# When the next field is split: eleven of the fields' halves moved within the row before their own

## The chip, the cores and the metric

The kernel runs on one core of one Trainium2 chip. The metric is the device time of one execution in microseconds, given as the median of several runs; one further execution of the same program was profiled instruction by instruction.

## The reference

The input is `r_inputs`, 1024 samples x 32 fields x 128 values, and `W`, one 128 x 128 matrix for each of the 496 pairs of fields (i, j) with i < j. All are 32-bit floats.

```python
v_i = inputs[:, I_IDX, :]
v_j = inputs[:, J_IDX, :]
transformed = jnp.einsum('bpd,ped->bpe', v_i, W)
return transformed * v_j
```

For each pair, field i is multiplied by the pair's matrix, and the product by field j, element by element. The output has 1024 x 496 x 128 values, 260 MB, against some 49 MB that are read.

## The kernel before

Pairs are numbered q in an order that goes by rows: field i = 30 comes first with its one pair, then i = 29 with two, down to i = 0 with 31. "Row i" below means the 31 - i pairs whose first field is i; `first_q[i]` is the number of its first pair. A pair is worked in two halves of 512 samples; u = 2q + half counts them.

Rows 30 to 26 (the first 15 pairs) are computed by one 32-bit matmul each half (line 212). In all others each factor is split into a coarse part and a rest, so that three fast matmuls give a half: `wh` with `xh` and `wl` with `xl` (line 215), and `wd` with `xd` (line 224), which is added three halves later (`LAG`). Between them ScalarE scales what has been accumulated (line 216). VectorE multiplies the result by field j into the output tile `ot` (line 230).

The splits are made while the kernel runs:

- A weight split (`split_w`, for two pairs) is one instruction on ScalarE (line 127) and three on GpSimd (lines 128, 129, 130).
- A field split (`split_x`, for half a field) is one on ScalarE (line 144, `xh`), and on GpSimd lines 145 and 146 (`xl`) and, for fields 9 to 0, line 150 (`xd`). For fields 25 to 10, `xd` is made on VectorE instead, five pairs later (line 269).

The order is written out by hand, and each engine works through its own instructions in that order. A list, `todo`, holds every split with the pair from which it may be issued and the pair by which it's due; it is sorted by the due pair. After each pair the first entry that may be issued is issued, one at a time (lines 260 to 264). A weight split may be issued from five pairs ahead of its use. A half of field i may be issued from `first_q[i + 1] + 1`, the beginning of the row before its own, and is due at `first_q[i]`:

```python
todo.append(((c - 3) * WC + 1, max(c * WC, nq0), lambda u, c=c: split_w(c, u)))
```

A weight split becomes due at every second pair, and those stand first in the list, so the two halves of a field take the two next free places: for field 5, pairs 302 and 304, with one weight split between them. Its row begins at pair 325, and the row in which it is split, row 6, at 300. The split tiles `xh`, `xl`, `xd` have two buffers each: field i is written over field i + 2.

Output goes out in tiles of four pairs, 2 MB each, issued by ScalarE's queue (line 259) two halves after the tile's last multiplication. There are three tiles of their own (`s0` to `s2`), and up to four more, which are the places of the four groups of late fields (`g0` to `g3`) for as long as these aren't loaded. A group of four fields (2 MB) is loaded at pairs 52, 141, 219 and 313 (line 108), and its place isn't used for output from 20 pairs before that; from pair 293 on three tiles are left. VectorE may write a tile again when its store has landed.

Weights come in chunks of eight pairs (512 KB) into three buffers, some by SyncE's queue alone (line 118), 25 of them in two parts, by GpSimd's queue (line 102) and SyncE's (line 103). A very small DMA (`mark`, line 99) follows these on GpSimd's queue. Field 0 is loaded at pair 421 into a weight buffer (line 90).

Of the kernel before, what the change touches and what calls it, by code (L numbers as in the profile page):

```python
# [12 lines left out]
NF = 32  # L13
# [7 lines left out]
NATIVE = 5  # L21
SHARED = 16
XDLAG = 10
LAG = 3
WB = 3
WLEAD = 12
XAFTER = 54
# [18 lines left out]
def kernel(  # L46
# [27 lines left out]
    spool = ctx.enter_context(tc.tile_pool(name="xs", bufs=2))  # L74
    rpool = ctx.enter_context(tc.tile_pool(name="wr", bufs=WB))
    wpool = ctx.enter_context(tc.tile_pool(name="ws", bufs=4))
# [5 lines left out]
    def load_x(f, pieces=1, eng=None):  # L82
        if f == 0:

            t = rpool.tile([P, WL, P], F32, tag="w", name="x_0").rearrange("p q e -> p (q e)")
        else:
            t = xpool.tile([P, BT], F32, tag=f"x{f}", name=f"x_{f}")
        s = BT // pieces
        for k in range(pieces):
            (eng or nc.sync).dma_start(out=t[:, k * s : (k + 1) * s], in_=xt[f, :, k * s : (k + 1) * s])  # L90
        x_sb[f] = t
# [20 lines left out]
    def load_w(c, splits=(0, WL), eng=nc.sync):  # L112
        w_raw[c] = rpool.tile([P, WL, P], F32, tag="w", name=f"w_{c}")
        if c in WAPART:
            load_apart(w_raw[c], wt[c])
            return
        for a, b in zip(splits, splits[1:]):
            eng.dma_start(out=w_raw[c][:, a:b, :], in_=wt[c, :, a:b, :])
# [19 lines left out]
    def split_x(f, a, u):  # L138

        if a == 0:  # L140
            x_s[f] = [spool.tile([P, BT], F32R, tag=t, name=f"{t}_{f}") for t in ("xh", "xl", "xd")]
        s = slice(a, a + HB)
        h, l, d = [t[:, s] for t in x_s[f]]
        nc.scalar.mul(h, x_sb[f][:, s], 1.0 - 2.0**-13)  # L144
        nc.gpsimd.tensor_tensor(l, x_sb[f][:, s], h.bitcast(F32), ALU.subtract)  # L145
        nc.gpsimd.tensor_scalar(l, l.bitcast(F32), 1.0 / EPS, 1.0, ALU.mult, ALU.mult)  # L146
        if f > NF - 2 - NATIVE - SHARED:
            later.append((min(u + XDLAG, 2 * first_q[f] + LAG - 1), d, h.bitcast(F32), l.bitcast(F32)))
        else:
            nc.gpsimd.tensor_tensor(d, h.bitcast(F32), l.bitcast(F32), ALU.subtract)  # L150
# [3 lines left out]
    first_q = {i: q for q, (i, j) in reversed(list(enumerate(pairs)))}  # L154
# [3 lines left out]
    todo = []  # L158
    for c in range(c0, nchunk):
        todo.append(((c - 3) * WC + 1, max(c * WC, nq0), lambda u, c=c: split_w(c, u)))  # L160
    for i in range(NF - 2 - NATIVE, -1, -1):
        for a in range(0, BT, HB):
            todo.append((first_q[i + 1] + 1 if i < NF - 3 - NATIVE else 2, first_q[i], lambda u, i=i, a=a: split_x(i, a, u)))
    todo.sort(key=lambda t: t[1])

    load_w(0, (0, 1, WL), nc.sync)
# [10 lines left out]
    w_at = {}  # L177
    for c in range(WB, -(-NQ // WL)):
        free = (c - WB + 1) * WL if (c - WB) * WL < nq0 else 0
        early = 0 if XAFTER < c <= XAFTER + WB else WLEAD - 6  # L180
        if c not in WAPART:
            w_at[max(c * WL - 3 * WC - 5 - early, free)] = c
    x_at = XAFTER * WL - 11
    assert x_at not in w_at and len(w_at) == NQ // WL - WB - len(WAPART)

# [32 lines left out]
    def second(u):  # L218
        q, h = divmod(u, 2)
        i, j = pairs[q]  # L220
        r = slice(q % WC * P, (q % WC + 1) * P)
        s = slice(h * HB, (h + 1) * HB)
        if q >= nq0:
            nc.tensor.matmul(  # L224
                po[u], w_s[q // WC][2][:, r], x_s[i][2][:, s], start=False, stop=True, skip_group_check=True
            )
        g, k = divmod(q, OG)
        if k == 0 and h == 0:
            ots[g] = out_tile(g)
        nc.vector.tensor_tensor(ots[g][:, k, s], po.pop(u), x_sb[j][:, s], ALU.mult)  # L230
        if q >= NQ - 2:
            stores.append((u + SLAG, out[g, :, k, s], ots[g][:, k, s]))
        elif g == 0 or q >= NQ - OG:
            if h == 1:
                stores.append((u + SLAG, out[g, :, k], ots[g][:, k]))
        elif k == OG - 1 and h == 1:
            stores.append((u + SLAG, out[g], ots[g]))

    for u in range(2 * NQ + LAG + SLAG):
        q = u // 2  # L240
        if u < 2 * NQ:
            i, j = pairs[q]
# [11 lines left out]
            if u == 2 * x_at + 1:  # L254
                load_x(0)
        if LAG <= u < 2 * NQ + LAG:
            second(u - LAG)
        while stores and stores[0][0] <= u - LAG:
            nc.scalar.dma_start(*stores.pop(0)[1:])
        if u % 2 == 1:  # L260
            ready = [t for t in todo if t[0] <= q]
            if ready:
                ready[0][2](u)
                todo.remove(ready[0])
        if w_next and (XAFTER if w_next[0] == XAFTER + 2 else w_next[0] - WB) in spent:
            load_w(w_next.pop(0))
# [36 lines left out]
```

## Time and profile before

| what | value |
|---|---|
| median of 5 runs | 750.47 us (748.31 to 752.86) |
| profiled execution | 749.89 us, span 748.1 us |
| mean granted TensorE clock | 0.986 |
| HBM read, written | 49.29 MB, 260.05 MB |
| mean rate over the span | 414 GB/s |
| store of an output tile, issue to landing (median) | 12.4 us |
| ScalarE, scaling (line 216), mean | 583 ns, 962 times |
| VectorE, output (line 230), mean | 685 ns, 720 times |
| VectorE, `xd` (line 269), mean | 948 ns, 32 times |
| ScalarE, `xh` (line 144), mean | 630 ns, 32 times |
| GpSimd, `xl`, second step (line 146), mean | 694 ns, 52 times |
| GpSimd, `xd` (line 150), mean | 1289 ns, 20 times |

The span goes from the first instruction to the last; the execution has 1.8 us around it. In the profile PE is TensorE's matmuls, PEld its weight loads, DVE is VectorE, ACT ScalarE, POOL GpSimd and SP SyncE; L128 is line 128 of the kernel. A group of instructions is shown with its busy time and the mean of one in ns, then the idle time of its engine just before, and who ended that. In a timeline and in the chain of waits the first number is the start and the second the length, both in us. Matmuls are pipelined: one is shown with 0.39 us, and the next starts 0.23 us after it.

The time of a pair in the trace: row 12 ends at 288.6 us, row 7 at 454.0, row 6 at 495.4, row 2 at 651.6, row 1 at 697.4.

### The profile page before, as it was taken

What the parts mean: (1) busy time and instruction counts of PE and PEld (TensorE: products, weight loads), DVE (VectorE), ACT (ScalarE), POOL (GpSimd) and SP (SyncE); (2) the same over time, 40 slices, a digit from 0 to 9 for tenths busy, and PEclk for the clock granted to TensorE, in tenths of its full rate; (3) what the DMA queues carried; (4) which work ended last, traced back from release to release, by engine and by line L of the source; (5) the groups of instructions that cost most, each with busy time, mean ns of one, the idle gap of its engine ahead of it and who ended that gap; (6) DMA issues with size and microseconds to landing.
All of it is one profiled execution on the core that took longest, in us unless ns stands there. A gap on an engine that the chain in (4) does not pass through costs nothing.

```text
span 748.1 us, 11063 instructions
## 1 busy us (share of the span) xinstructions
PE 700.7 (94%) x2946; PEld 555.3 (74%) x2946; DVE 669.2 (89%) x1024; ACT 626.1 (84%) x1256; POOL 615.3 (82%) x902
## 2 busy tenths in 40 slices
PE   7998999899999999998999989889999999999993
PEld 3576777687787788776787777668788787877882
DVE  4899999899999999986999979789899998888894
ACT  1298989799999999886898878789899898978993
POOL 1789999999999999896988878778888979797660
PEclk9999999999999999999999999999999999999998
DMA  9999999999999999999999999999999999999998
GB/s 346 423 428 427 424 428 428 419 395 419 415 420 420 424 426 424 424 426 416 426 428 423 429 416 396 407 428 407 423 416 421 408 429 406 418 393 402 419 424 328
DMA packets 32941, 310.06 MB, mean 414 GB/s; under 512 B 5104, under 2 KB 5232, under 8 KB 16752
## 3 DMA queue, kind: packets, MB, share of 16 engines
q10 hardware_dynamic: 19584, 261.10, 83.0%
q1 hardware_dynamic: 8864, 36.77, 12.5%
q0 software_dynamic: 4432, 11.48, 4.2%
q8 instruction: 24, 0.39, 0.2%
q14 instruction: 37, 0.30, 0.1%
HBM read 49.29 MB, written 260.05 MB: 414 GB/s over the span
## 4 chain that ended last, share of the span: by engine, by line
PE 72%; DMA 13%; POOL 8%; DVE 3%; issue 1%; ACT 1%; DVEq 0%; ACTq 0%; POOLq 0%
PE po L215 46%; PE po L224 23%; DMA out_dram<-ot 12%; PE po L212 4%; DVE ot L230 3%; POOL wl L128 2%; POOL xd L150 2%; POOL xl L145 1%; POOL wd L130 1%; POOL xl L146 1%; ACT po L216 1%; DMA x<-in_xt_dram 1%; POOL wd L129 1%; DVE xd L269 0%; ACT wh L127 0%
## 5 line engine op out<-in xcount | busy, mean ns | idle before, releaser
L216 ACT ACTIVATE po<-po 128x512 f32<-128x512 f32 x962 | 545.7, 583 | 89.8 <-PE po L215 50.8
L230 DVE TENSOR_TENSOR ot<-po,x 128x512 f32<-128x512 f32 x720 | 467.9, 685 | 47.4 <-DMA out_dram<-ot 21.4
L215 PE MATMUL po<-xl,wl 128*128 128x512 f32 x962 | 379.5, 395 | 20.1 <-POOL wl L128 18.8
L215 PE MATMUL po<-xh,wh 128*128 128x512 f32 x962 | 378.8, 394 | 9.9 <-DVE ot L230 9.8
L224 PE MATMUL po<-xd,wd 128*128 128x512 f32 x962 | 377.1, 392 | 1.8 <-DVE xd L269 1.8
L215 PEld LDWEIGHTS po<-xl,wl 128*128 128x128 f32 x962 | 182.1, 189 | 66.5 <-POOL wl L128 27.1
L128 POOL TENSOR_TENSOR wl<-w,wh 128x256 fp32r<-128x256 f32 x241 | 184.2, 764 | 47.2 <-ACT wh L127 42.9
L215 PEld LDWEIGHTS po<-xh,wh 128*128 128x128 f32 x962 | 182.1, 189 | 53.0 <-DVE ot L230 14.4
L224 PEld LDWEIGHTS po<-xd,wd 128*128 128x128 f32 x962 | 182.1, 189 | 40.8 <-ACT po L216 2.4
L230 DVE TENSOR_TENSOR ot<-po,x_g 128x512 f32<-128x512 f32 x272 | 176.7, 687 | 21.4 <-PE po L224 14.2
L130 POOL TENSOR_TENSOR wd<-wl,wd 128x256 fp32r<-128x256 f32 x241 | 179.3, 744 | 20.1
L129 POOL TENSOR_SCALAR wd<-wh 128x256 fp32r<-128x256 f32 x241 | 99.1, 411 | 20.5
L127 ACT ACTIVATE wh<-w 128x256 fp32r<-128x256 f32 x241 | 99.3, 412 | 6.0 <-DVE ot L230 5.2
L145 POOL TENSOR_TENSOR xl<-x_g,xh 128x512 fp32r<-128x512 f32 x32 | 41.6, 1301 | 5.0 <-DVE ot L230 4.6
L146 POOL TENSOR_SCALAR xl<-xl 128x512 fp32r<-128x512 f32 x52 | 36.1, 694 | 4.6
L145 POOL TENSOR_TENSOR xl<-x,xh 128x512 fp32r<-128x512 f32 x20 | 26.6, 1330 | 15.7 <-ACT xh L144 15.5
L212 PE MATMUL po<-x,w 128*128 128x512 f32 x60 | 29.4, 652 | 4.1 <-DMA x<-in_xt_dram 4.1
L269 DVE TENSOR_TENSOR xd<-xh,xl 128x512 fp32r<-128x512 f32 x32 | 30.3, 948 | 0.2 <-POOL xl L146 0.2
L212 PEld LDWEIGHTS po<-x,w 128*128 128x128 f32 x60 | 12.1, 207 | 20.6 <-issue 13.3
L150 POOL TENSOR_TENSOR xd<-xh,xl 128x512 fp32r<-128x512 f32 x20 | 25.8, 1289 | 1.7
L144 ACT ACTIVATE xh<-x 128x512 fp32r<-128x512 f32 x20 | 12.4, 627 | 11.4 <-DMA x<-in_xt_dram 11.3
L144 ACT ACTIVATE xh<-x_g 128x512 fp32r<-128x512 f32 x32 | 20.2, 630 | 0.0
(7 smaller groups left out, 33.9 us busy)
## 6 DMA issues: line engine op xcount, KB each, us to landing
out_dram<-ot ACTq DMA_DIRECT2D x122, 2048.0 KB, 12.4
w<-in_wt_dram SPq DMA_DIRECT2D x36, 512.0 KB, 10.5
w<-in_wt_dram POOLq DMA_DIRECT2D x25, 448.0 KB, 11.3
x_g<-in_xt_dram SPq DMA_DIRECT2D x4, 2048.0 KB, 18.1
x<-in_xt_dram SPq DMA_DIRECT2D x14, 512.0 KB, 8.9
out_dram<-ot ACTq DMA_DIRECT2D x6, 512.0 KB, 8.8
w<-in_wt_dram SPq DMA_DIRECT2D x26, 64.0 KB, 5.9
x<-in_xt_dram ACTq DMA_DIRECT2D x4, 256.0 KB, 6.0
```

The source lines that it names most:

```text
L127: nc.scalar.mul(h, raw, 1.0 - 2.0**-13)
L128: nc.gpsimd.tensor_tensor(l, raw, h.bitcast(F32), ALU.subtract)
L129: nc.gpsimd.tensor_scalar(d, h.bitcast(F32), EPS, 1.0, ALU.mult, ALU.mult)
L130: nc.gpsimd.tensor_tensor(d, l.bitcast(F32), d.bitcast(F32), ALU.subtract)
L145: nc.gpsimd.tensor_tensor(l, x_sb[f][:, s], h.bitcast(F32), ALU.subtract)
L146: nc.gpsimd.tensor_scalar(l, l.bitcast(F32), 1.0 / EPS, 1.0, ALU.mult, ALU.mult)
L150: nc.gpsimd.tensor_tensor(d, h.bitcast(F32), l.bitcast(F32), ALU.subtract)
L212: nc.tensor.matmul(po[u], w_raw[q // WL][:, q % WL, :], x_sb[i][:, s], start=True, stop=True)
L215: nc.tensor.matmul(po[u], w_s[c][t][:, r], x_s[i][t][:, s], start=t == 0, stop=t == 1)
L216: nc.scalar.mul(po[u], po[u], 1.0 + EPS)
L224: nc.tensor.matmul(po[u], w_s[q // WC][2][:, r], x_s[i][2][:, s], start=False, stop=True, skip_group_check=True)
L230: nc.vector.tensor_tensor(ots[g][:, k, s], po.pop(u), x_sb[j][:, s], ALU.mult)
```

## The change

Until now every half of a field might be issued from one pair after the beginning of the row before its own. Now, for fields 11 to 1, the first half may be issued a fifth of that row later, and the second three fifths of it (a row of `NF - 2 - i` pairs, rounded down). Fields 25 to 12 and field 0 are as before. The due pair, which sets the order of the list, is unchanged, as are the splits themselves.

```diff
+SPREAD = 12
...
-            todo.append((first_q[i + 1] + 1 if i < NF - 3 - NATIVE else 2, first_q[i], lambda u, i=i, a=a: split_x(i, a, u)))
+            at = first_q[i + 1] + 1 if i < NF - 3 - NATIVE else 2
+            if 0 < i < SPREAD:
+                at += (NF - 2 - i) * (1 + 2 * (a > 0)) // 5
+            todo.append((at, first_q[i], lambda u, i=i, a=a: split_x(i, a, u)))
```

The pairs at which the two halves are issued, for some of the fields:

| field | row before begins | own row begins | before | after |
|---|---|---|---|---|
| 11 | 171 | 190 | 172, 174 | 176, 184 |
| 8 | 231 | 253 | 232, 234 | 236, 246 |
| 5 | 300 | 325 | 302, 304 | 306, 316 |
| 3 | 351 | 378 | 352, 354 | 358, 368 |
| 1 | 406 | 435 | 408, 410 | 412, 424 |
| 0 | 435 | 465 | 436, 438 | 436, 438 |

## The prediction

> **What bounds the kernel now.** I read the page, then the windows, the waits and the chain stretch by stretch, then GpSimd's timeline at a row's beginning. First the page:
>
> ```profile
> PE 700.7 (94%) x2946; PEld 555.3 (74%) x2946; DVE 669.2 (89%) x1024; ACT 626.1 (84%) x1256; POOL 615.3 (82%) x902
> GB/s 346 423 428 427 424 428 428 419 395 419 415 420 420 424 426 424 424 426 416 426 428 423 429 416 396 407 428 407 423 416 421 408 429 406 418 393 402 419 424 328
> L128 POOL TENSOR_TENSOR wl<-w,wh 128x256 fp32r<-128x256 f32 x241 | 184.2, 764 | 47.2 <-ACT wh L127 42.9
> ...
> L145 POOL TENSOR_TENSOR xl<-x_g,xh 128x512 fp32r<-128x512 f32 x32 | 41.6, 1301 | 5.0 <-DVE ot L230 4.6
> ```
>
> Two limits lie close together. TensorE is 94% busy, and the DMA moves up to 428 GB/s; I take 426 as its full rate. An output tile (four pairs) and its share of the weights are 2.097 + 0.262 = 2.359 MB, which is 5.54 us at 426. Unhindered compute issues a store every 5.38 to 5.50 us (stores at 510.86, 516.24, 521.74, 527.12 in ScalarE's timeline), 5.44 on average. So the question is where a TensorE stall costs anything. The windows divide the second half:
>
> ```profile
> 355.00:449.00 94.00, 88.63 (x380) 71.85 (x379) 85.04 (x128) 81.31 (x163) 80.79 (x120) 0.98 1.01 425
> 449.00:488.00 39.00, 35.02 (x153) 28.37 (x153) 31.69 (x48) 32.52 (x66) 32.18 (x49) 1.00 0.99 401
> 488.00:651.00 163.00, 156.13 (x683) 127.37 (x683) 148.34 (x229) 145.99 (x294) 138.75 (x208) 1.00 1.01 418
> ```
>
> The columns are the stretch, its length, busy time of TensorE, its weight loads, VectorE, ScalarE and GpSimd, granted clock, DMA share, GB/s. To 449 the DMA is full. From 449 on, where only three output tiles are left, it runs at 401 and 418: there compute is late. The waits of 488 to 650 and the chain of 488 to 651 say what makes it late:
>
> ```profile
> PE po L215 <- POOL wl L128: 5.8, 4, 1.8
> ```
>
> ```profile
> 500.69 1.27 POOL xl L145
> 502.04 0.63 POOL xl L146
> 502.75 1.29 POOL xd L150
> 504.04 0.69 POOL wl L128
> 504.78 0.50 PE po L215
> ```
>
> After one DMA piece that ends at 488.7 the longest pieces of this chain are TensorE and GpSimd alone. Four times, once a row, the chain leaves TensorE for GpSimd's split of the next field. The four gaps in TensorE's timeline are 1.08 (at 503.7), 1.17 (540.5), 1.81 (580.0) and 1.79 us (620.2). GpSimd's own timeline shows the first:
>
> ```profile
> 495.28 1.30 POOL L145 TENSOR_TENSOR xl<-x_g,xh 128x512 fp32r<-128x512 f32 x1
> 496.67 0.62 POOL L146 TENSOR_SCALAR xl<-xl 128x512 fp32r<-128x512 f32 x1
> 497.38 1.30 POOL L150 TENSOR_TENSOR xd<-xh,xl 128x512 fp32r<-128x512 f32 x1
> 498.63 0.74 POOL L128 TENSOR_TENSOR wl<-w,wh 128x256 fp32r<-128x256 f32 x1
> 499.46 0.41 POOL L129 TENSOR_SCALAR wd<-wh 128x256 fp32r<-128x256 f32 x1
> 499.95 0.74 POOL L130 TENSOR_TENSOR wd<-wl,wd 128x256 fp32r<-128x256 f32 x1
> 500.65 1.31 POOL L145 TENSOR_TENSOR xl<-x_g,xh 128x512 fp32r<-128x512 f32 x1
> ```
>
> A field half takes 498.63 - 495.28 = 3.35 us, a weight split 2.02, and a weight split is due every 5.44/2 = 2.72. So GpSimd has 0.70 to spare per weight split; each half makes the weights 3.35 - 0.70 = 2.65 late, two with one weight split between them 5.30. TensorE waited 1.08 here, so the weights' lead covers about 4.2.
>
> **The change, part by part.** Nothing is added or removed. In the built program 22 halves move (fields 11 to 1): ScalarE's L144, GpSimd's L145 and L146, for fields 9 to 1 its L150, and for 11 and 10 two VectorE instructions of L269 each. The order on TensorE and on SyncE's queue is the same, and so are the bytes.
>
> *GpSimd.* In the new order at least four weight splits stand between the halves of each of fields 9 to 1. Four give back 4 x 0.70 = 2.8 us, more than the 2.65 that a half costs, so the weights are never 5.30 late, but 2.65. GpSimd's queue also has its own DMA issues, 0.62 us each for a weight chunk (L102) and 0.63 for the small mark (L99); some fall next to a moved half. Both at once: 2.65 + 0.62 + 0.63 = 3.90, still under 4.2. If that cover were short by 0.3, 18 halves would cost 5.4 us together; I take nothing. The weight chunk that waits behind a half is issued at most 3.35 us later; the page has these chunks landing 11.3 us after issue, and the chunk goes to the buffer of the third one before it, 18 pairs (24 us) ahead of its first split. Nothing follows.
>
> *The new deadline.* The second half is issued at three fifths of the row. For field 1, 30 - 18 = 12 pairs are left, for field 11 eight: 8 x 1.36 = 10.9 us against 3.35 + 2.65. The cover is 4.9 us.
>
> *ScalarE and VectorE.* A half's L144 takes 0.63 us (the page's mean) in a queue with L216 behind it. In row 12 (265 to 289), with both halves at the row's beginning, TensorE was busy 24.00 of 24.00 us; single halves ask less. The same row covers L269, whose mean is 0.95.
>
> *Fields 11 to 6, before 449: nothing.* Rows 9 to 7 have TensorE gaps of 1.01, 1.16 and 1.16 us (361.6, 392.9, 427.0), but stores there land 13.9 to 16.6 us after issue. One store is 2.097 MB / 426 = 4.9 us, so about two lie ahead of it. At 439 the tiles for output fall from four to three and VectorE waits 4.0 us for a store; an earlier compute waits longer for the same landing. The gain is 0, at most the DMA's shortfall, 94 x (426 - 425)/426 = 0.2.
>
> *Field 5, 449 to 488.* A gap of 1.16 us (465.1) goes. The chain again ends in a DMA wait at 488, so it's worth only what the DMA catches up: all of 39 x (426 - 401)/426 = 2.3 us at most, 0 at least. The stretch holds two things that stay: the dip after the halved clock at 444, and the start of the group load (L108, issued at 466.6). I take 0.8.
>
> *Fields 4 to 1, 488 to 651: the term that counts.* From the store at 486.88 to that at 652.91 are 29 stores in 166.03 us. Compute alone would need 29 x 5.44 = 157.8, the DMA (29 x 2.359 + 0.524 for x_0)/0.426 = 161.7. Whichever is longer rules: 166.0 - 161.7 = 4.3 us gained. Its ends: with the DMA at 430, 160.2 and 5.8 gained; at 419, which is what it reached from 512 to 540 with TensorE busy 28.00 of 28.00, 164.4 and 1.6.
>
> *After 651.* Field 0 stays, and with it the gap of 1.81 us at 660.4. Up to that point the DMA moved 163 us x 418 GB/s = 68.1 MB; now 163 - 4.3 = 158.7 us at 426 move 67.6, so 0.5 MB more lies ahead. From 651 to 742 it moved 91 us x 408 = 37.1 MB; 37.6 in the same 91 us are 413 GB/s, which it can do. The gain passes through.
>
> *What speaks against it.* TensorE's gaps don't vanish, some move into longer waits for stores at 441.9 (2.04 us now) and 479.9 (2.82). The granted clock halved four times, after gaps of 1.99, 3.70, 2.04 and 1.81 us, and did not after 2.82, 1.81 and 1.79 (its mean is 0.72 in 442 to 448 and in 660 to 666, 1.00 in 479 to 484). Three windows of 10 us with a halving read 0.83: (1 - 0.83) x 10 = 1.7 us of clock lost, 3.4 us at half. I reckon with one more, at 480, where almost all of it is hidden by queued stores: 0.5.
>
> The Trainium skill (TensorE: Matmul & The Clock Gate, Part 1: The HAM clock gate) says that the clock falls to half after an idle window of about 3.4 us. The length agrees with the 3.4 of this trace; the threshold doesn't, since 1.81 was enough once. By the rule the gap at 480 would grow to 2.82 + 1.16 = 3.98 and halve for certain, and the gaps at 580 and 620 could never have done so; by the trace either is chance.
>
> **Sum.** 0 + 0.8 + 4.3 - 0.5 = 4.6 us. The profiled execution took 749.89 (its span 748.1, and 1.8 around it): 745.3. The median of the five runs is 750.47, 0.6 higher: 745.9.
>
> **Rivals.** *The DMA gives no more than now.* For: 419 GB/s in 512 to 540, without a stall; scattered chunk loads may set that rate. Against: 425 over 355 to 449, with the same loads. Gain 1.6 + 0 - 0.3: 749.2, with 747.5 to 751 around it. That the splits don't separate, say because another wait holds GpSimd, would give 750.5 and counts here; the gaps all follow a pair of halves, which speaks against it.
>
> *Slower: the clock.* With compute ahead, every hitch of the DMA ends in a TensorE gap. Each halving takes 1.7 us, and in 449 to 742 stores are queued for one at a time. The 4.6 us are used up by 4.6/1.7 = 2.7 halvings that aren't hidden; from five on the kernel is slower by 5 x 1.7 - 4.6 = 3.9: 754.4. For: gaps of 1.81 have sufficed. Against: only two group loads and one fall in tiles make long gaps after 300; a queue that is 5.54 against 5.44 makes gaps of 0.1 us.
>
> **How the numbers follow.** The forecast has 0.60, the unchanged DMA rate 0.25, the clock 0.15. The time is the forecast's, 745.9, its own range 742.9 (2.3 + 5.8 gained, less 0.5) to 748. To hold eight in ten the range takes in the second case and the way to the third: 742.9 to 752.0. About 0.5% (3.75 us) is what a measurement of this kernel can tell from no change. Faster by more: 0.60; within: 0.25; slower by more: 0.15.
>
> **What would show it.** Right: from 488 to 651 no TensorE wait on L128 but that of field 0 afterwards, stores 5.5 us apart, more VectorE waiting on stores, 424 GB/s or more, GpSimd's halves apart by four weight splits. The gap at 660 stays; the wait at 441 grows by some 3 us without any cost. Wrong: new waits on L128 in the middle of rows, DMA at 418 in spite of even stores, or more than five halved stretches.

## The result and the profile after

The changed kernel takes 748.54 us (median of 52 runs, 745.12 to 753.15) against 751.20 for the kernel before (94 runs, 746.42 to 756.38; its first five had 750.47). The ratio is 0.9972, with a 95% interval of 0.9962 to 0.9981: 2.1 us faster (1.4 to 2.9), where 4.6 were forecast. The sign was right and the size about half or less. Single executions spread over 8 us and more, and the two profiled ones don't show the gain: the one before had a span of 748.1 us, the one after 748.8 (750.59 as a whole). So the traces are used for how the work runs, and the ratios for how long it takes.

The page of the changed kernel; its lines 129 and 146 are 128 and 145 of the one before:

```profile
PE 703.5 (94%) x2946; PEld 557.7 (74%) x2946; DVE 665.3 (89%) x1024; ACT 625.8 (84%) x1256; POOL 614.7 (82%) x902
GB/s 347 422 428 427 430 425 429 420 396 423 420 419 424 426 424 424 427 419 420 428 425 425 421 417 394 424 406 414 417 417 411 420 416 417 398 404 379 405 431 344
L129 POOL TENSOR_TENSOR wl<-w,wh 128x256 fp32r<-128x256 f32 x241 | 183.6, 762 | 54.2 <-ACT wh L128 49.9
```

GpSimd has the same work and now idles longer in front of it, because it's ahead: line 129 waited 49.9 us for ScalarE, not 42.9. GpSimd's timeline in row 5 shows why. The two halves of field 4 stand apart, and the first has a small DMA issue directly before it:

```profile
504.29 0.63 POOL L100 DMA_DIRECT2D mark<-in_xt_dram  x1
504.95 1.30 POOL L146 TENSOR_TENSOR xl<-x_g,xh 128x512 fp32r<-128x512 f32 x1
...
508.29 0.76 POOL L129 TENSOR_TENSOR wl<-w,wh 128x256 fp32r<-128x256 f32 x1
...
518.38 1.30 POOL L146 TENSOR_TENSOR xl<-x_g,xh 128x512 fp32r<-128x512 f32 x1
```

The waits of 488 to 650 in the changed kernel:

```profile
DVE ot L234 <- DMA out_dram<-ot: 19.5, 18, 2.4
POOL wl L129 <- ACT wh L128: 16.3, 18, 5.0
PEld po L219 <- DVE ot L234: 8.4, 12, 1.7
```

TensorE's waits for the weight split, 5.8 us before, are gone. In their place VectorE waits 19.5 us for stores to land. In the kernel before it had waited 8.1 there:

```profile
DVE ot L230 <- DMA out_dram<-ot: 8.1, 10, 1.9
```

The chain of 488 to 651 says the same; its first line is the share of each line of the kernel:

```profile
by line: DMA out_dram<-ot 46.7%; PE po L219 23.5%; DVE ot L234 14.0%; PE po L228 11.1%; issue 1.5%; POOL wd L131 0.9%; ACT po L220 0.8%; ACT wh L128 0.7%; POOL wl L129 0.4%; POOL wd L130 0.2%; DVEq L234 0.2%; ACTq L220 0.0%; POOLq L129 0.0%
...
515.60 11.90 DMA out_dram<-ot
527.62 3.69 DVE ot L234 x6
532.53 12.22 DMA out_dram<-ot
544.87 9.77 DVE ot L234 x16
```

Before, the DMA had 9.8% of this chain, all of it in one piece at the beginning, and then TensorE and GpSimd set the pace:

```profile
by line: PE po L215 56.0%; PE po L224 27.6%; DMA out_dram<-ot 9.8%; POOL xd L150 4.0%; POOL wl L128 3.0%; POOL xl L145 2.4%; issue 1.9%; POOL xl L146 1.5%; POOL wd L130 1.4%; POOL wd L129 0.8%; DVE ot L230 0.4%; POOL w L102 0.4%; ACT wh L12
...
472.57 16.03 DMA out_dram<-ot
```

Now a store lands, VectorE writes its tile, and the next store is waited for. The bound has moved to the stores, and these are no faster. The windows, with the same columns as before:

```profile
355.00:449.00 94.00, 89.20 (x387) 73.09 (x386) 85.97 (x129) 82.83 (x167) 82.76 (x123) 0.98 1.01 424
449.00:488.00 39.00, 34.22 (x142) 27.80 (x141) 30.13 (x47) 30.08 (x61) 30.69 (x46) 0.91 1.01 409
488.00:651.00 163.00, 159.37 (x690) 128.21 (x689) 140.51 (x228) 147.03 (x296) 139.33 (x209) 1.00 1.00 414
```

From 488 to 651 the DMA moves 414 GB/s, less than the 418 of before, although compute now waits for it and not the other way round. The forecast took 426.

### The profile page after: what moved, and what is told of

Same layout as the page of the kernel before. It is cut to its first block, busy times and chain, and to the rows that moved or that the text cites. A ratio compares the mean times of both kernels' runs of the same rounds, so it can differ in the third digit from the quotient of the medians.

```text
span 748.8 us, 11065 instructions
## 1 busy us (share of the span) xinstructions
PE 703.5 (94%) x2946; PEld 557.7 (74%) x2946; DVE 665.3 (89%) x1024; ACT 625.8 (84%) x1256; POOL 614.7 (82%) x902
## 4 chain that ended last, share of the span: by engine, by line
PE 60%; DMA 24%; DVE 7%; POOL 5%; issue 1%; ACT 1%; DVEq 0%; ACTq 0%; POOLq 0%
PE po L219 39%; DMA out_dram<-ot 22%; PE po L228 19%; DVE ot L234 7%; POOL wl L129 2%; PE po L216 2%; DMA w<-in_wt_dram 2%; POOL wd L131 1%; POOL xl L146 1%; ACT po L220 1%; DVE xd L273 1%; DMA x<-in_xt_dram 1%; POOL xl L147 1%; POOL wd L130 0%; POOL xd L151 0%
## 5 line engine op out<-in xcount | busy, mean ns | idle before, releaser
L129 POOL TENSOR_TENSOR wl<-w,wh 128x256 fp32r<-128x256 f32 x241 | 183.6, 762 | 54.2 <-ACT wh L128 49.9
L234 DVE TENSOR_TENSOR ot<-po,x_g 128x512 f32<-128x512 f32 x272 | 177.2, 687 | 12.1 <-DMA out_dram<-ot 7.4
L216 PEld LDWEIGHTS po<-x,w 128*128 128x128 f32 x60 | 11.9, 205 | 20.4 <-issue 12.6
```

Source lines behind the costliest of these rows:

```text
L129: nc.gpsimd.tensor_tensor(l, raw, h.bitcast(F32), ALU.subtract)
L216: nc.tensor.matmul(po[u], w_raw[q // WL][:, q % WL, :], x_sb[i][:, s], start=True, stop=True)
```

## The experiments

Counting VectorE's multiplications in a trace gives the time at which each pair begins. For the kernels that the argument turns on (us from the beginning of the span):

| kernel | pair 296 | pair 324 | pair 436 | 324 to 436 | end of span |
|---|---|---|---|---|---|
| before | 448.8 | 494.2 | 653.0 | 158.8 | 748.1 |
| changed | 448.2 | 493.4 | 654.1 | 160.7 | 748.8 |
| changed, profiled again (e11) | 449.3 | 494.7 | 654.2 | 159.5 | 749.1 |
| changed, fields 5 to 1 alone (e1) | 448.8 | 496.9 | 654.4 | 157.5 | 748.4 |
| before, groups in parts (e9) | 448.1 | 493.7 | 653.3 | 159.6 | 746.1 |
| changed, groups in parts (e7) | 450.3 | 495.8 | 652.3 | 156.5 | 746.3 |
| fields 5 to 1 alone, groups in parts (e10) | 449.1 | 494.0 | 650.0 | 156.0 | 744.2 |
| changed, no late chunk in two parts (e13) | 450.4 | 493.3 | 652.9 | 159.6 | 747.4 |
| before, a sixteenth not stored (e14) | 448.5 | 493.2 | 652.2 | 159.0 | 745.5 |
| changed, a sixteenth not stored (e15) | 448.4 | 492.1 | 644.1 | 152.0 | 735.6 |

Compute alone would take 112 pairs x 5.44/4 us = 152.3 from 324 to 436. Each row of the table is one profiled execution.

**The two parts of the change alone (e1, e2).**

```diff
-            if 0 < i < SPREAD:
+            if 0 < i < 6:          # e1
+            if 5 < i < SPREAD:     # e2
```

> Only fields 5 to 1 are split later; fields 11 to 6 at the beginning of the row, as before. Theory (a GpSimd stall costs nothing while stores queue four tiles deep): same as the whole change, 0.997 of before, since all that counts lies after 449 us. Rival (every removed stall gives its share): three of the eight gaps of 9.3 us in sum, those of rows 9 to 7 with 3.3 us, come back, so about a third of the gain goes: 0.998.

> The other part alone: only fields 11 to 6 are split later. Theory: 1.000 of before (within 0.001), with the three gaps at 362, 393 and 427 us gone and the wait for a store at 440 us longer by some 2 to 3 us. Rival (every removed stall gives its share): 0.999. If the longer wait at 440 costs clock, it is slower, 1.001 to 1.002.

Measured: 0.9998 (0.9977 to 1.0019) with the late fields alone, 0.9996 (0.9974 to 1.0019) with the early ones. For e2 that is what the theory said: the gaps of rows 9 to 7 are gone, and TensorE's gap before the store at 440 is 6.4 us, not 2.0. For e1 it's a miss: 0.997 was expected and lies just outside the interval. In its profile the wait at the last group load had become a TensorE gap of 6.1 us, and pair 324 began at 496.9, 2.7 later than before. That made the group load the first suspect.

**Is the time of the stalls real? A quarter of the late stores left out (e3, e4).**

```diff
-            stores.append((u + SLAG, out[g], ots[g]))
+            n = OG - 1 if g > 80 else OG
+            stores.append((u + SLAG, out[g, :, :n], ots[g][:, :n]))
```

> The kernel before, but from the tile of pair 324 on only three of its four pairs are stored, so the output lacks a quarter from there. The DMA then has 1.84 MB for 5.44 us of compute, 4.3 us at 426 GB/s, and no longer sets the pace. Theory: compute alone rules, the four gaps on L128 of rows 5 to 2 stay (5.9 us), stores 5.44 us apart plus these; 29 tiles in 163.7 us.

> The changed kernel with the same stores left out (three of four pairs from pair 324 on). Theory (the stalls were real, and the DMA takes the gain back): here the gain is paid out, 29 tiles in 157.8 us, the whole 5.5 to 6 us faster than the lightened kernel before, over twice the 2.1 us of the full kernels. Rival (the stalls were never worth more than 2 us): the two lightened kernels lie 2 us apart too.

Measured: 0.9952 (0.9930 to 0.9975) for the kernel before, 0.9824 (0.9793 to 0.9856) for the changed one; their medians are 747.41 and 736.98, 10.4 us apart. The same change that pays 2.1 us pays 10 where the DMA has less to do. So the stalls cost time that can be won, the stores take most of the gain back, and the rival falls. The 10.4 are more than the 5.5 to 6 expected. In e3's profile TensorE waits 6.0 us for the weight split from 488 to 650, and once 3.9 us, at 485, with a halved clock behind it; e4 has neither.

**Is it the number of tiles? (e5, e6)** In e5 the fourth output tile is given up earlier; in e6 there are six tiles of two pairs.

```diff
+    until["g0"] = 231                       # e5, on the changed kernel
...
-OG = 4                                      # e6, on the changed kernel
+OG = 2
-    used = {... enumerate(("s0", "s1", "s2", *sorted(until, reverse=True)))}
+    used = {... enumerate(("s0", "s1", "s2", "s3", "s4", "s5", *sorted(until, reverse=True)))}
```

> The changed kernel with the fourth output tile given up at pair 231 and not at 293. Theory (with three tiles the DMA gets no more than about 414 GB/s however early compute is): the stretch from 355 to 449 us falls from 424 to 413 to 418 GB/s and takes 1.5 to 3 us more; the waits for stores come in rows 9 to 7 already, and that at 440 us gets shorter. Time 1.002 to 1.004 above the changed kernel. Rival (the late stretch is slow because of something else in it): 355 to 449 stays at 424 and the time with it.

> The changed kernel with output tiles of two pairs, six where there were three, in the same memory; a store is 1 MB with rows of 8 KB. Theory (stores are held back by tiles that are written whole and freed whole): more stores queue at once, 488 to 651 us goes from 414 to 420 GB/s or more, waits for stores fall, 0.990 to 0.994 of before. Rival (the DMA's rate is that of its traffic): 414 stays or falls, since the rows are shorter, 0.997 or slower.

Measured: e5 1.0007 (0.9986 to 1.0027), which is 0.0035 above the changed kernel, as expected, and its window from 355 to 449:

```profile
355.00:449.00 94.00, 93.55 (x404) 76.95 (x403) 87.19 (x134) 86.40 (x173) 81.81 (x120) 0.98 0.99 411
```

The last number, 411 GB/s, looks like the expected fall, but isn't one. The stretch begins behind a TensorE gap of 9.4 us; from 355 to 371 the DMA moved 350 GB/s, and from 371 to 449 it moved 423, with three tiles and with stores that landed 10.9 us after issue (median). Three tiles alone don't hold the DMA down, and the theory as it was put falls. e6 is slower, 1.0037 (1.0017 to 1.0056): its rows of 8 KB got 413 GB/s from 488 to 651. More and smaller stores are no remedy.

**Is the gain lost at the group load? (e7, e9, e10)** Each group of four fields is loaded field by field, five pairs apart, on the changed kernel (e7), the kernel before (e9), and the changed one with only fields 5 to 1 split later (e10).

```diff
-            if u % 2 == 0 and q in group_at:
-                load_group(group_at[q])
+            if u % 2 == 0 and q in part_at:
+                load_group(*part_at[q])
...
+    part_at = {q - 15 + 5 * m: (k, m) for k, q in enumerate(XAT) for m in range(XG)}
```

> The changed kernel with each group of four late fields loaded field by field, five pairs apart, the last where the whole was loaded. Theory (the long TensorE gap at the group load halves the clock and costs what the early compute has won): the gap of 4.8 us at 478 us falls below 2, no halving follows it, 0.993 to 0.995 of before. Rival (the halving is hidden by queued stores, as the prediction reckoned): within 0.001 of the changed kernel.

> The kernel before, with each group loaded field by field, and the splits at the row's beginning. Theory (the change's gain was lost at the group load, where a longer wait halves the clock and lets the DMA run dry): the parts alone bring little, 0.998 to 1.000 of before, and with them the change is worth 4 us or more (0.9932 with both). Rival (the parts are worth 3 us by themselves and the change its 2 us besides, the two don't meet): 0.996.

> Groups in parts, and only fields 5 to 1 split later. Theory (an earlier compute only lengthens the wait for a store at 440 us, and a longer TensorE gap there lets the clock stay halved for longer): the gap at 440 falls from 5.2 to about 2 us and the halving from 6.8 to 3.4 us, 0.991 to 0.993 of before. Rival (the early fields' stalls cost nothing and save nothing): 0.993 as with all eleven fields.

Measured: e7 0.9932 (0.9908 to 0.9957), e9 0.9962 (0.9939 to 0.9985), e10 0.9914 (0.9882 to 0.9947). e7 alone seemed to settle it: parts bring 3 us, and no halving follows the last group load. But e9 has the parts without the change and brings 0.0038 too, so with parts the change is worth 0.9932/0.9962 = 0.9970, as without. That is what the rival said, that the two gains add up. It isn't settled: the interval of this quotient, worked out from the two, goes from about 0.994 to 1.000. And the late fields alone speak for the theory: they're worth 0.9914/0.9962 = 0.9952 with parts (about 0.991 to 0.999) and 0.9998 without (e1). So do the windows of e9, e7 and e10, in this order:

```profile
488.00:651.00 163.00, 155.96 (x675) 127.61 (x676) 151.54 (x229) 144.30 (x290) 136.95 (x206) 0.99 1.00 413
488.00:651.00 163.00, 161.00 (x698) 129.54 (x697) 141.26 (x233) 148.27 (x299) 141.48 (x213) 1.00 1.01 423
488.00:651.00 163.00, 161.05 (x697) 129.75 (x698) 142.42 (x234) 147.89 (x299) 141.06 (x211) 1.00 1.01 422
```

With parts, the changed kernels pass from pair 324 to 436 in 156.5 and 156.0 us, against 159.6 without the change. The sum of the prediction at 426 GB/s, for these 28 tiles, is (28 x 2.359 + 0.524)/0.426 = 156.3. Without parts the change had no gain there in its two profiles. Whether the group load takes a part of the gain stays open.

e10 has the lowest time of the complete kernels, some 6 us below before, and is faster than the changed kernel. That late fields alone are better than all eleven is what the theory of the wait at 440 expected (TensorE's gap there was 3.1 us and no clock was lost, against 5.2 and a halving in e7), but the two intervals overlap.

Both edits at once, with small tiles (e8), were no better than small tiles alone:

> Small tiles and groups in parts together, on the changed kernel. If both theories hold, 0.985 to 0.990 of before; if either falls, no better than the better one of the two alone.

Measured: 1.0053 (1.0024 to 1.0082).

**The changed kernel again (e11).**

> The changed kernel itself, on the chip of the two others: 0.997 of before, with a TensorE gap over 4 us at the load of the last group (about 478 us) and the clock halved behind it.

Measured: 0.9971 (0.9949 to 0.9993), with gaps of 5.8 us at 438 and 4.1 at 480, each followed by a halved clock. Its chain from 500 to 650 has the stores in front too (50.7% in the first profile over the same stretch):

```profile
by line: DMA out_dram<-ot 57.9%; PE po L219 17.9%; DVE ot L234 12.9%; PE po L228 8.2%; issue 2.8%; ACT wh L128 1.2%; ACT po L220 1.2%; POOL wd L131 1.0%; POOL wl L129 1.0%; POOL xl L146 0.9%; POOL xd L151 0.9%; POOL wd L130 0.5%; POOL xl L1
```

**Does the slowest DMA engine set the rate? (e12, e13)** Every DMA leaves sixteen landing marks in the trace. In the profile of the changed kernel thirteen of a late store's sixteen come close together, and three come late: for the store issued at 630.4, thirteen after 6.9 to 8.2 us and the others after 10.5, 10.7 and 12.3. (In e11, the same kernel, it's mostly one or two that come late.) The last one counts for VectorE: the store of 515.60 has its last mark after 11.9 us, at 527.5, and VectorE goes on at 527.62. From 495 to 640 the mean spread between the first and the last mark is 4.8 us (4.9 in e11, 3.3 before). The Trainium skill (DMA: Bandwidth & Descriptors, Why a DMA increments its semaphore by 16 and not by 1) explains the marks: each of the engines counts up once its own part has landed, and only all sixteen mean that the data is there. The experiments are meant to move rows between engines, by loading more weight chunks in two parts, or none; which engine takes which row can't be read in these traces.

```diff
-WAPART = tuple(range(12, 62, 2))
+WAPART = tuple(range(12, 36, 2)) + tuple(range(36, 54)) + (54, 56, 58, 60)   # e12
+WAPART = tuple(range(12, 36, 2))                                             # e13
```

> The changed kernel with nearly every weight chunk from the 36th on (pair 288) loaded in two parts, not every second; the larger part goes in 112 rows of 4 KB over fourteen places, so that two of the sixteen DMA engines get less. Theory (a store lands when the slowest of sixteen does, 3.5 us after the median one, and that is what VectorE waits for): the spread between first and last landing of a store, mean 4.8 us from 495 to 650 in the changed kernel, changes by 1 us or more, down if those two are the slow ones, and the DMA's rate there follows it: down to 3 us, 420 GB/s or more and 0.993 to 0.995 of before; up to 6 us, below 412 and 1.000. Rival (the rate is that of a short queue, whichever engine is last): spread may move, rate stays at 414 to 418, time within 0.001 of the changed kernel.

> The opposite: from the 36th chunk on none is loaded in two parts, so all sixteen engines get the same rows. Theory: the spread moves the other way than with more chunks apart, up to 6 us or more if the spared engines are the slow ones, the DMA falls to 410 GB/s or less from 488 to 651 us, 1.000 to 1.004 of before. Rival (short queue): within 0.001 of the changed kernel, 0.997; it has 9 GpSimd DMA issues less, which is worth nothing by both.

Measured: e12 0.9999 (0.9972 to 1.0025), e13 0.9975 (0.9952 to 0.9998). The spread from 495 to 650 was 4.3 us in e12 and 4.1 in e13, so it fell a little in both, and the rates went apart:

```profile
488.00:651.00 163.00, 158.01 (x677) 127.00 (x676) 143.07 (x228) 145.04 (x290) 145.39 (x220) 0.99 1.00 407
```

```profile
488.00:651.00 163.00, 160.69 (x688) 127.42 (x687) 140.28 (x231) 147.12 (x296) 132.44 (x197) 1.00 1.01 423
```

The first is e12, where GpSimd's further DMA issues also brought back a stall on the weight split (2.3 us at 601, behind a `mark` that waited 2.4 us for the one before it); the second is e13, as fast as the changed kernel. Spread and rate don't go together as the theory had it, and the rates left the rival's 414 to 418 as well. Nor is the rate of this window the pace: e13 has 423 GB/s and takes 159.6 us from pair 324 to 436, e11 has 418 and takes 159.5. That the slowest engine sets the landing is seen in the marks; that it sets the rate is not shown.

**How close is the floor? A sixteenth of the late stores left out (e14, e15).**

```diff
-            stores.append((u + SLAG, out[g], ots[g]))
+            n = OG - 1 if g > 80 and g % 4 == 0 else OG
+            stores.append((u + SLAG, out[g, :, :n], ots[g][:, :n]))
```

> The kernel before, from pair 324 on with every fourth tile stored by three of its four pairs; the output lacks a sixteenth from there. On average 2.23 MB go out and in per tile, 6% less, which is 5.33 us at 418 GB/s against 5.44 of compute. Theory (the store traffic is the floor, a few per cent above compute): stalls stay and set the pace, 0.996 to 0.999 of before.

> The changed kernel with the same sixteenth left out. Theory (store traffic is the floor, and only just): 6% less of it, and compute rules, so 5 us or more lie between this and the same lightening of the kernel before, 0.987 to 0.992 of before; the spread of a store's landings from 495 to 640 us falls from 4.8 to 2 us or less. Rival (something else takes the gain, that the quarter also relieved): the two stay 2 us apart, 0.994 to 0.996.

Measured: e14 0.9971 (0.9949 to 0.9992), e15 0.9851 (0.9827 to 0.9874); medians 748.38 and 738.45, 9.9 us apart. The chains from 488 to 651, first e14:

```profile
by line: PE po L215 59.0%; PE po L224 29.3%; POOL xd L150 3.2%; POOL wl L128 2.6%; POOL xl L145 1.6%; issue 1.6%; POOL wd L130 0.9%; POOL xl L146 0.8%; POOL wd L129 0.5%; POOL w L102 0.4%; ACT wh L127 0.3%; POOLq L128 0.1%; ACT po L216 0.0%
```

and e15, with its window below it:

```profile
by line: PE po L219 66.9%; PE po L228 33.3%
```

```profile
488.00:651.00 163.00, 163.00 (x720) 134.63 (x719) 152.65 (x241) 153.82 (x310) 145.98 (x217) 1.00 1.01 415
```

In e15 nothing but TensorE is left on the chain. It is busy for 163.00 of 163.00 us, pairs 324 to 436 take 152.0 us, which is compute alone. The DMA moves 415 GB/s here because compute asks for no more: (28 x 2.228 + 0.524) MB in 152.0 us are 414 GB/s. With all stores the same pace would ask for (28 x 2.359 + 0.524) MB, 438 GB/s, and the best slice on the page of the changed kernel has 431. In e14 the same sixteenth brings 2 us, and TensorE's stalls behind GpSimd still set the pace (6.0 us of waits for the weight split from 488 to 650; e15 has none). What these runs don't tell apart is a limit of the DMA's rate and one of the three tiles: with less to store a tile also comes back sooner (10.4 us from issue to landing in e15, 12.1 in the changed kernel). Of the 9.9 us, the trace has 1.1 before pair 324 (493.2 - 492.1) and 7.0 from 324 to 436 (159.0 - 152.0). The rest comes after 436, where the clock halved once in e14 behind the gap at 660 (a granted mean of 0.83 from 660 to 670) and not in e15 (1.00 from 652 to 662). The spread of landings fell to 3.0 us, not to the 2 that was expected, and 0.9851 is a little below the 0.987 to 0.992 expected.

## Why the prediction was wrong in size

*GpSimd.* Right in each step. The halves stand apart, no weight split is late from 488 to 651, the deadline of the next row costs nothing, and even a half that follows a DMA issue is covered. The gap of field 0 stays (1.5 us at 661). That the stalls were worth nearly 6 us in rows 5 to 2 fits e15 against e14: 6.0 us of waits for the weight split are gone, and pairs 324 to 436 take 7.0 us less.

*Fields 11 to 6: nothing.* Right; e2 measured 0.9996. The wait at 440 grew as forecast (VectorE's 4.0 us became 6.2 in row 7).

*Fields 4 to 1: the step that failed.* It was put as the longer of compute (157.8 us for 29 stores) and the DMA, and the DMA was priced at 426 GB/s: 161.7 us, 4.3 gained (161.8 without rounding on the way). The structure was right and the rate wrong for this kernel. The prediction read the 418 GB/s of this stretch as a sign that compute was late; the changed kernel, whose compute waits for the stores, gets 414 (418 in e11). From the store at 488.45 to that at 653.68 its 29 stores take 165.2 us, against 166.0 before: 0.8 gained in this pair of profiles. The sum of the prediction with 418 would have been 68.9/0.418 = 164.8, a gain of 1.2. The row for that stood in the prediction: 419 GB/s in 512 to 540, with TensorE busy throughout. It was put at the edge of the range and made a rival, because 355 to 449 has 425. The rate had to be taken from the stretch to which it was applied. Even so, 414 to 418 isn't a limit of the stretch: with groups in parts the same change reached 422 and 423 there, and the pace that the prediction's 426 gives.

*Field 5, 449 to 488: 0.8, less 0.5 for the clock.* The halving at 480 came, in both profiles of the change. Pair 324 begins 0.8 earlier in one of them and 0.5 later in the other, so the net of 0.3 isn't told from nothing.

*The rival "the DMA gives no more than now"* had 749.2, 1.3 us below before; that is the mechanism that came. The measured 2.1 us lie between it and the forecast. The profiled pair has no gain, so where the 2.1 us of the medians arise can't be pointed out in a trace.

*The clock as the way to a slower kernel.* The longer gaps and halvings came. Between 400 and 700 us the clock halved twice before (at 444 and 662, 6.8 us in all) and three times in the changed kernel (at 443, 481 and 679, 13.6 us in all); 482 to 492 had a granted mean of 0.73. They didn't make it slower than before.

What stays open is why the DMA gives 414 to 418 GB/s here and 422 to 425 elsewhere. Longer queues of stores don't explain it: e5 had 423 with stores that landed after 10.9 us, sooner than the 12.1 here. Nor do three tiles alone (e5, e7 and e10 have three as well), small tiles or the rows of the weight chunks. The load of the last group, just ahead of the stretch, is the suspect that isn't cleared. A fourth tile to the end wasn't tried.

## What to carry to other kernels

Where two limits lie within a few per cent, a stall that is removed is paid out only down to the other limit, so that limit's rate is the number to get right. Take it from the stretch where it will bind, not from the best one on the page. To see whether a stall is real, relieve the other limit a little in the kernel with and without the change: a sixteenth of the stores made 2 us into 10.

## What the runs showed of the hardware

A DMA share of 1.00 doesn't mean full speed. From 488 to 651 the sixteen engines of the changed kernel are busy at a share of 1.00 with 414 GB/s, from 355 to 449 at 1.01 with 424; in e12 a share of 1.00 goes with 407.

The sixteen parts of a store don't land together. In the changed kernel the spread between first and last grows from 3.6 us (stores issued from 488 to 530) to 5.6 (610 to 650), more than a whole store takes at 426 GB/s (4.9 us); in e13 from 2.3 to 5.0. In e9, where compute sets the pace, it doesn't grow (3.0 and 1.9), and with a quarter of the stores left out it's 1.0 to 1.2 on the mean from 495 to 640. That a few engines fall behind where the stores set the pace is a reading of these means; in e12 it doesn't grow either (4.3 and 2.5). The Trainium skill (DMA: Bandwidth & Descriptors, Latency and other measured facts) says that engines 7 and 15 are usually slower than the others. These traces don't number the engines; the profile of the changed kernel shows three late ones, e11 mostly one or two.

The clock's halving follows no single length of gap: 1.8 us of idle TensorE at 660 were followed by a halved clock (before) and 3.1 at 441 were not (e10, whose clock stayed full to the end of its work).
